# Writing a batch's projection of messages behind the first block of the next batch's messages

## The chip, the cores and the metric

The kernel runs on one core of one Trainium2 chip. The metric is the device time of one execution in microseconds (us); it was measured in three runs of the kernel before. A profile of one further execution shows where that time lies. Engines are named as in the profile: PE is TensorE's matrix unit, PEld its weight loads, DVE the vector engine, ACT the scalar engine, POOL GpSimd, and SP the engine that only issues transfers here.

## The reference, cut to what matters

Four graph layers run over 16 batches of 1024 nodes with 256 features. The change lies in the first one:

```python
m_t = jnp.einsum('uv,bud->bvd', A_m, h_t) * h_t
a_t = jnp.einsum('buv,bud->bvd', S * A_a, h_t)
z_t = beta1 * h_t + beta2 * (jnp.einsum('bvd,de->bve', a_t, Wa) + ba) \
    + beta3 * (jnp.einsum('bvd,de->bve', m_t, Wm) + bm)
```

`m_t` are the messages: a product with the adjacency matrix and then an elementwise product with `h_t`. `S` are scores of the edges, computed from `pre_u` and `pre_v`, two products of `h_t` with halves of `W1`. The term `beta1 * h_t + beta3 * m_t Wm` needs no scores; the kernel computes it ahead of all that does.

## The kernel before, in words

The nodes lie in 8 tiles of 128 partitions, the features in 2 halves of 128. A preparation (to about 103 us) loads the adjacency matrix and makes the edge sides of batches 0 to 3. Then follows the score-free part (generator `score_free`, to about 952 us), in which the change lies, and after it four groups of four batches with the remaining layers.

The score-free part goes over the batches b = 0 to 15. For each of them there are up to four pieces of work on PE:

- `edge_sides` (for b from 4): 8 node tiles, each with a product of 512 columns and one of 256 columns for each feature half, weights `hT`. PE's result lies in two PSUM banks, ACT copies them to `st` (L331, L332), and SP issues three stores for each pair of tiles (L337, L338). `st` has two buffers.
- `messages`: four blocks (feature half dh, node half v), each of 8 products with a bank of 512 columns, 64 matrix instructions in all. Behind each block DVE multiplies the bank by `hT` into `mT` (L351).
- the next batch's input: for b + 1 up to 3 two loads, `h` and its transposed form `hT` (L288, L297); for b + 1 from 4 a load of `h` (L288) and `turned`: 16 transposes on PE into four banks (L308), copied to `hT` in turns by DVE (L139) and ACT (L141). The first bank (v = 0, dh = 0) is copied by DVE, the second (v = 0, dh = 1) by ACT, the third by DVE, the fourth by ACT.
- `without_edges`, the projection: four banks, each of 2 products with weights `wm` and moving operand `mT` (16 matrix instructions), DVE adds `beta1 * hT` into `zb` (L366), and SP stores `zb`, 1 MB (L368). Its first two banks need the blocks of `mT` with v = 0, which are the first and the third; its last two need the second and the fourth.

The order on PE within a batch is thus edge sides, messages, transposes for the next batch, projection; then come the next batch's edge sides. The code is a generator; each `yield` gives an estimate of PE's time since the last one. The helper `Side.along` hands out steps of another generator, `score_steps`, in proportion to it (0.26 steps for each us in this part). A score step is a gather of 512 KB on POOL (L706), two operations on DVE (L823, L825), four on ACT (L829), and one or two scatters on POOL (L711). The first of its DVE operations waits for a matrix product a few instructions back (`paced`), so that the scores can't run ahead of PE. The clearing of a table (32 MB of zero writes, ACT's transfer queue) is also spread over the yields.

The tiles `h` and `hT` share a pool of 5 buffers, `mT` and `zb` one of 4, the PSUM banks one of 8. A buffer goes to the next tile of its pool in order of request. Tile's scheduler sets the order of each engine's instructions from the order of the code, the dependences and a model of times, so loads can stand earlier in SP's queue than in the code.

Of the kernel before, what the change touches and what calls it, by code (L numbers as in the profile page):

```python
# [68 lines left out]
def gnn_stack_kernel(  # L69
# [41 lines left out]
    def bank():  # L111
        return psum[-1].tile([P, HN], F32, tag="bank", name="bank")
# [8 lines left out]
    def paced(ins, back=6):  # L121


        if recent:
            after(tc, ins, [recent[max(0, len(recent) - back)]], mybir.DependencyClass.Sync, "keeps pace")
        return ins

    def product(*args, **kw):
        recent.append(nc.tensor.matmul(*args, **kw))  # L129
        del recent[:-BACK]  # L130
        return recent[-1]
# [15 lines left out]
    def load_wm(pool, queue):  # L147

        wm = pool.tile([P, DH, D], F32, name="wm")
        queue.dma_start(wm, g0_Wm.rearrange("(c p) k -> p c k", p=P))  # L150
        nc.vector.tensor_scalar(wm, wm, beta3, None, ALU.mult)
        return wm

    def load_w1(pool, queue):

        w = pool.tile([P, DH, 3, D], F32, name="w1")
        for s, a in enumerate((g0_W1[:D], g0_W1[D:], g0_Wa)):
            queue.dma_start(w[:, :, s, :], a.rearrange("(c p) k -> p c k", p=P))
        return w

    def with_beta2(w):
        return nc.vector.tensor_scalar(w[:, :, 2, :], w[:, :, 2, :], beta2, None, ALU.mult)
# [54 lines left out]
    def turn_adj(stage):  # L217

        for jt in range(0, NT, 2):
            st = stage(2 * N)  # L220
            for k in range(2):
                for v in range(NV):
                    ps = bank()
                    for c in range(HT):
                        it = v * HT + c
                        nc.tensor.transpose(
                            ps[:, c * P : (c + 1) * P], adj_sb[:, it, (jt + k) * P : (jt + k + 1) * P], ident
                        )
                    evacuate(st[:, k * N + v * HN : k * N + (v + 1) * HN], ps)
                yield 1.2  # L230
            nc.sync.dma_start(
                adjT_d[jt : jt + 2].rearrange("t p v -> p t v"), st.rearrange("p (t v) -> p t v", t=2)
            )

    def load_naturals(stage):

        t = stage(3 * DH * D).rearrange("p (i c k) -> p i c k", i=3, c=DH)
        for i, a in enumerate((g1_W, gat2.W1, gat3.W1)):
            nc.sync.dma_start(t[:, i], a.rearrange("(c p) k -> p c k", p=P))
        return t  # L240
# [43 lines left out]
    def load_h(pool, b, pieces=1):  # L284
        h = pool.tile([P, NT, D], F32, tag="wide", name="h")
        n = NT // pieces
        for t in range(0, NT, n):
            nc.sync.dma_start(h[:, t : t + n, :], x[b, t * P : (t + n) * P].rearrange("(t p) d -> p t d", p=P))  # L288
        return h

    def node_pairs(t):
        return t.rearrange("p (h n) -> p h n", h=DH)

    def load_kept(pools, b):
        h = load_h(pools[0], b)
        hT = node_pairs(pools[0].tile([P, DH * N], F32, tag="wide", name="hT"))
        nc.sync.dma_start(hT.rearrange("p h n -> p (h n)"), hT_d[b])  # L297
        return h, hT
# [41 lines left out]
    def messages(pools, h, hT):  # L340
        mT = node_pairs(pools[1].tile([P, DH * N], F32, tag="wide", name="mT"))
        for dh in range(DH):
            for v in range(NV):
                cols = slice(v * HN, (v + 1) * HN)
                ps = bank()
                for ut in range(NT):
                    product(
                        ps, h[:, ut, dh * P : (dh + 1) * P], adj_sb[:, ut, cols],
                        start=ut == 0, stop=ut == NT - 1,
                    )  # L350
                nc.vector.tensor_tensor(mT[:, dh, cols], ps, hT[:, dh, cols], ALU.mult)  # L351
                yield 6.9
        return mT

    def without_edges(pools, b, hT, mT, wm):

        zb = node_pairs(pools[1].tile([P, DH * N], F32, tag="wide", name="zb"))
        for v in range(NV):
            cols = slice(v * HN, (v + 1) * HN)
            for eh in range(DH):  # L360
                ps = bank()
                for dh in range(DH):
                    product(
                        ps, wm[:, dh, eh * P : (eh + 1) * P], mT[:, dh, cols], start=dh == 0, stop=dh == DH - 1,
                    )
                nc.vector.scalar_tensor_tensor(zb[:, eh, cols], hT[:, eh, cols], beta1, ps, ALU.mult, ALU.add)  # L366
            yield 3.4
        nc.sync.dma_start(zb_d[b], zb.rearrange("p h n -> p (h n)"))  # L368
# [4 lines left out]
    with ExitStack() as stack:  # L373
# [56 lines left out]
        def clear():  # L430

            if zeros:
                paced(nc.scalar.dma_start(zeros.pop(0), zero))
# [252 lines left out]
    with tc.If(listed > 0) as arm:  # L686
        with ExitStack() as stack:
# [214 lines left out]
            def load_gd(g, v, ut, **pace):  # L902
                view = dense[g % BUFS][:DUMP].rearrange("(t p v) b -> t p v b", p=P, v=N)
                gd = gd_pool.tile([P, QN, GB], F32, tag="gd", name="gd")
                ins = nc.sync.dma_start(gd, view[ut][:, v * QN : (v + 1) * QN, :])
                put[g].before(paced(ins, **pace))
                return gd

            def load_hw(b):
                hw = node_major("hw")  # L910
                nc.sync.dma_start(hw, hw_d[b].rearrange("p (t d) -> p t d", t=NT))
                return hw
# [14 lines left out]
            with ExitStack() as first:  # L927
                own1 = first.enter_context(tc.tile_pool(name="own1", bufs=1, reuse_waits="tile"))
                st_pool = first.enter_context(tc.tile_pool(name="st", bufs=2, reuse_waits="tile"))
                side = Side(score_steps(own1))  # L930
                pools = (wide_t, wide_z)
                next_up = load_kept(pools, 0)
                wm = load_wm(own1, nc.sync)
                zero = own1.tile([P, ZERO], F32, name="zero")
                nc.gpsimd.memset(zero, 0.0)

                def stage(n):
                    return st_pool.tile([P, 2 * 3 * D], F32, tag="st", name="stage")[:, :n]

                def score_free():  # L940
                    yield from turn_adj(
                        lambda n: wide_z.tile([P, DH * N], F32, tag="wide", name="stage")
                    )
                    h, hT = next_up
                    for b in range(B):
                        if b == 1:
                            nat = load_naturals(stage)
                            w1 = load_w1(own1, nc.sync)
                        if b == 2:
                            paced(with_beta2(w1))  # L950
                        if b >= GB:
                            yield from edge_sides(st_pool, b, w1, hT)
                        if b == B - 1:
                            first_hw.extend(load_hw(i) for i in range(GB - 1))
                            first_gd.extend(load_gd(0, 0, ut) for ut in range(4))
                        mT = yield from messages(pools, h, hT)
                        now = hT

                        if b + 1 < GB:
                            h, hT = load_kept(pools, b + 1)  # L960
                        elif b + 1 < B:
                            h = load_h(pools[0], b + 1)
                            hT = turned(pools[0], h)
                            yield 2.4
                        yield from without_edges(pools, b, now, mT, wm)
                        if b == 1:
                            prepare(nat)
                            yield 3

                def with_zeros(main):  # L970
                    for n, us in enumerate(main):
                        if 7 < n < 40 or n > 40 and n % 3 == 0:
                            clear()
                        yield us

                side.along(with_zeros(score_free()))
                assert not zeros

# [439 lines left out]
    with arm.Else():  # L1418
        with ExitStack() as stack:
# [7 lines left out]
            w1, wm = load_w1(own, nc.scalar), load_wm(own, nc.scalar)  # L1427
# [80 lines left out]
            with tc.For_i(0, B, 1) as b:  # L1508
                h = load_h(wide, b)
                hT = turned(wide, h)  # L1510
# [35 lines left out]
```

## Time and profile before

| | us |
|---|---|
| three runs: lowest, median, highest | 3159.90, 3167.11, 3171.89 |
| the profiled execution | 3164.07 |
| its span | 3162.6 |
| PE busy | 3092.3 (98%) |
| DVE busy | 2360.7 (75%) |
| ACT busy | 1945.9 (62%) |
| POOL busy | 1876.9 (59%) |

An engine's busy time is the sum of its instructions, overlaps taken once. PE is busy nearly all of the time, so a time of PE without an instruction is what has to be looked for, and next to it what PE waited for. In lists of groups a line gives the line of the program, the engine, the operation with its tiles, the count, the busy time and the mean of one in ns, and then the idle time just before the group's instructions with what released them. In the timeline a line is a stretch of like instructions: its start, its length, and in brackets the idle time before it. All products of the score-free part are issued by one helper, so their line is L129 throughout, and they are told apart by their tiles: `adj_sb,h` are messages, `mT,wm` the projection, `w,hT` the edge sides, `ident,h` (L308) the transposes.

### The profile page before, as it was taken

What the parts mean: (1) busy time and instruction counts of PE and PEld (TensorE: products, weight loads), DVE (VectorE), ACT (ScalarE), POOL (GpSimd) and SP (SyncE); (2) the same over time, 40 slices, a digit from 0 to 9 for tenths busy, and PEclk for the clock granted to TensorE, in tenths of its full rate; (3) what the DMA queues carried; (4) which work ended last, traced back from release to release, by engine and by line L of the source; (5) the groups of instructions that cost most, each with busy time, mean ns of one, the idle gap of its engine ahead of it and who ended that gap; (6) DMA issues with size and microseconds to landing.
All of it is one profiled execution on the core that took longest, in us unless ns stands there. A gap on an engine that the chain in (4) does not pass through costs nothing. (4 is left out here: it accounts for less than half of the span.)

```text
span 3162.6 us, 39016 instructions
## 1 busy us (share of the span) xinstructions
PE 3092.3 (98%) x11954; PEld 2180.8 (69%) x11954; DVE 2360.7 (75%) x3191; ACT 1945.9 (62%) x6512; POOL 1876.9 (59%) x1483
## 2 busy tenths in 40 slices
PE   8999999999999999999999999999999999999999
PEld 5444554544547756888875688888568888858887
DVE  7887778677774678999677899976789982157844
ACT  3245556656667876776887677788767764414242
POOL 1156778676664577767666776766766760076600
PEclk9999999999999999999999999999999999999999
DMA  9988897888889777567877766787765655475500
GB/s 318 331 320 308 271 307 260 269 238 256 249 287 318 227 211 206 154 192 261 286 231 201 211 168 176 255 284 232 221 193 156 167 184 167 134 252 159 164 4 28
DMA packets 288420, 699.96 MB, mean 221 GB/s; under 512 B 46141, under 2 KB 141178, under 8 KB 281034
## 3 DMA queue, kind: packets, MB, share of 16 engines
q0 software_dynamic: 128224, 387.80, 42.0%
q1 hardware_dynamic: 132538, 258.46, 23.8%
q10 hardware_dynamic: 27440, 51.13, 4.3%
q8 instruction: 96, 1.57, 0.2%
q14 instruction: 122, 1.00, 0.1%
HBM read 565.83 MB, written 131.41 MB: 220 GB/s over the span
## 5 line engine op out<-in xcount | busy, mean ns | idle before, releaser
L829 ACT ACTIVATE z<-z 128x256 f32<-128x256 f32 x2432 | 979.0, 406 | 581.8 <-DVE z L825 521.7
L823 DVE TENSOR_TENSOR z<-z,u 128x1024 f32<-128x1024 f32 x608 | 739.9, 1222 | 388.2 <-PE bank L129 250.9
L129 PE MATMUL bank<-feats,m 128*128 128x257 f32 x4096 | 919.5, 382 | 16.1 <-DVE m L1093 10.9
L706 POOL DMA_INDIRECT z<-v_d,slot_v x512 | 654.6, 1278 | 405.1 <-ACT z L829 194.2
L129 PEld LDWEIGHTS bank<-feats,m 128*128 128x128 f32 x4096 | 768.8, 190 | 134.6 <-DVE m L1093 20.8
L711 POOL DMA_INDIRECT dense_d<-gt,slot_at x512 | 680.8, 1330 | 190.8 <-issue 136.2
L825 DVE SCALAR_TENSOR_TENSOR z<-z,w2r 128x1024 f32<-128x1024 f32 x608 | 738.6, 1221 | 9.0
L129 PE MATMUL bank<-gc,hw 128*128 128x256 f32 x2048 | 452.4, 382 | 11.0 <-ACT gc L1121 10.1
L829 ACT ACTIVATION_READ_ACCUMULATOR z<-z 128x1 f32 x2432 | 460.9, 190 | 0.0
L129 PE MATMUL bank<-adj_sb,h 128*128 128x512 f32 x1024 | 442.9, 593 | 3.3 <-DMA h<-in_x_dram 1.6
L129 PEld LDWEIGHTS bank<-gc,hw 128*128 128x128 f32 x2048 | 386.9, 191 | 76.1 <-ACT gc L1121 18.7
L1093 DVE SCALAR_TENSOR_TENSOR m<-rho,tau,adj_sb 128x512 f32<-128x512 f32 x512 | 376.7, 747 | 67.1 <-PE bank L129 64.4
L129 PE MATMUL bank<-adjT_in,y 128*128 128x512 f32 (+1 forms) x960 | 403.9, 581 | 6.1 <-DMA adjT_in<-adjT_d 2.8
L129 PEld LDWEIGHTS bank<-adj_sb,h 128*128 128x128 f32 x1024 | 194.5, 190 | 243.8 <-issue 240.5
L129 PE MATMUL bank<-w,hT 128*128 128x512 f32 (+1 forms) x1024 | 335.5, 488 | 0.9 <-ACT z L829 0.9
L129 PEld LDWEIGHTS bank<-adjT_in,y 128*128 128x128 f32 x960 | 182.0, 191 | 221.6 <-issue 204.5
L1121 ACT ACTIVATE gc<-gd 128x1024 f32<-128x1024 f32 x128 | 265.3, 2073 | 89.4 <-PE bank L129 70.2
L129 PEld LDWEIGHTS bank<-w,hT 128*128 128x128 f32 x1024 | 194.8, 191 | 142.9 <-issue 120.6
L129 PE MATMUL bank<-g_wT,z 128*128 128x257 f32 x1024 | 232.5, 381 | 2.5 <-issue 2.5
L129 PEld LDWEIGHTS bank<-g_wT,z 128*128 128x128 f32 x1024 | 193.2, 191 | 33.2 <-issue 6.3
L706 POOL DMA_INDIRECT z<-v_d,x_node x96 | 121.9, 1270 | 135.1 <-ACT z L829 79.9
L711 POOL DMA_INDIRECT dense_d<-gt,x_at x96 | 121.0, 1261 | 29.3 <-issue 27.1
(169 smaller groups left out, 2327.4 us busy)
## 6 DMA issues: line engine op xcount, KB each, us to landing
gd<-dense_d SPq DMA_DIRECT2D x128, 512.0 KB
dense_d<-zero ACTq DMA_DIRECT2D x64, 512.0 KB
adjT_in<-adjT_d SPq DMA_DIRECT2D x112, 256.0 KB
h<-in_x_dram SPq DMA_DIRECT2D x19, 1024.0 KB
u_d<-st SPq DMA_DIRECT2D x64, 256.0 KB
v_d<-st SPq DMA_DIRECT2D x64, 256.0 KB
hw_d<-st SPq DMA_DIRECT2D x64, 256.0 KB
u<-u_d POOLq DMA_DIRECT2D x32, 512.0 KB
```

What stands on the lines that cost most here:

```text
L129: recent.append(nc.tensor.matmul(*args, **kw))
L706: return nc.gpsimd.indirect_dma_start(out=dst, out_offset=None, in_=src[:], in_offset=bass.IndirectOffsetOnAxis(ap=at, axis=0), **how,)
L711: return nc.gpsimd.indirect_dma_start(out=dst[:], out_offset=bass.IndirectOffsetOnAxis(ap=at, axis=0), in_=src, in_offset=None,)
L823: paced(nc.vector.tensor_tensor(z, z, u, ALU.add))
L825: nc.vector.scalar_tensor_tensor(zk, zk, 0.0, w2r[:, None, :].to_broadcast([P, GB, D]), ALU.max, ALU.mult)
L829: nc.scalar.activation(zk[:, c, :], zk[:, c, :], AF.Copy, accum_out=s[:, k, c : c + 1])
L1093: nc.vector.scalar_tensor_tensor(m, r[:, cols], ta[:, jt : jt + 1], ea[:, jt, cols], ALU.max, ALU.mult)
L1121: paced(nc.scalar.activation(gc, gd.rearrange("p n i -> p i n"), AF.Copy), 16)
```

## The change

The generator of a batch's messages is now run to its first yield, that is through its first block. Then the projection of the batch before it is run in full, and then the other three blocks. A projection is only prepared in its own batch (a generator in the list `behind`) and is run in the next one; the last is run behind the loop. Operands and results are the same, and so are the numbers of instructions and transfers.

```diff
                     h, hT = next_up
+                    behind = []
                     for b in range(B):
...
-                        mT = yield from messages(pools, h, hT)
-                        now = hT
-
+                        steps = messages(pools, h, hT)
+                        yield next(steps)
+                        for last in behind:
+                            yield from last
+                        mT = yield from steps
+                        behind = [without_edges(pools, b, hT, mT, wm)]
                         if b + 1 < GB:
                             h, hT = load_kept(pools, b + 1)
                         elif b + 1 < B:
                             h = load_h(pools[0], b + 1)
                             hT = turned(pools[0], h)
                             yield 2.4
-                        yield from without_edges(pools, b, now, mT, wm)
                         if b == 1:
                             prepare(nat)
                             yield 3
+                    yield from behind[0]
```

## The prediction

> **What bounds the kernel now.** I read the page's busy times first, then PE's groups in the score-free part for what PE waited for, then PE's timeline there, and last what DVE and ACT do at the places where the order changes.
>
> ```profile
> PE 3092.3 (98%) x11954; PEld 2180.8 (69%) x11954; DVE 2360.7 (75%) x3191; ACT 1945.9 (62%) x6512; POOL 1876.9 (59%) x1483
> ```
>
> PE sets the time. What the change can win is idle time of PE in its own part, and the groups of that part (0 to 1010 us) give it:
>
> ```profile
> L129 PE MATMUL bank<-adj_sb,h 128*128 128x512 f32 x1024 | 442.9, 593 | 3.3 <-DMA h<-in_x_dram 1.6 <-ACT st L331 1.5
> L129 PE MATMUL bank<-w,hT 128*128 128x512 f32 x512 | 242.5, 596 | 0.0
> L129 PE MATMUL bank<-mT,wm 128*128 128x512 f32 x256 | 117.5, 611 | 10.2 <-DVE mT L351 10.2
> ```
>
> The projection (`mT,wm`) waited 10.2 us in all for DVE's product `mT`; the edge sides (`w,hT`), which come behind it, waited for nothing. PE's timeline shows where:
>
> ```profile
> 139.59 1.02 PE L129 MATMUL bank<-mT,wm 128*128 128x512 f32 x2
> 142.23 3.70 PE L129 MATMUL bank<-mT,wm 128*128 128x512 f32 x8 [1.61 <-DVE mT L351]
> 149.81 5.49 PE L129 MATMUL bank<-mT,wm 128*128 128x512 f32 x6 [3.88 <-DVE mT L351]
> 155.09 28.04 PE L129 MATMUL bank<-adj_sb,h 128*128 128x512 f32 x64
> ...
> 713.63 4.46 PE L129 MATMUL bank<-mT,wm 128*128 128x512 f32 x10
> 722.75 4.41 PE L129 MATMUL bank<-mT,wm 128*128 128x512 f32 x6 [4.67 <-DVE mT L351]
> ...
> 888.55 1.91 PE L308 MATMUL bank<-ident,h 128*128 128x128 f32 x16
> 890.30 7.03 PE L129 MATMUL bank<-mT,wm 128*128 128x512 f32 x16
> 897.17 20.80 PE L129 MATMUL bank<-w,hT 128*128 128x512 f32 x64
> ```
>
> Batch 0 waits twice, batch 11 once, the other 13 projections not at all: there PE goes from the transposes into the projection (7.03 us) and on into the edge sides without a gap. In those 7.03 us the copies of the new `hT` are made. For the batch turned at 888.55 DVE and ACT show them:
>
> ```profile
> 889.98 1.27 DVE L139 COPY hT<-bank 128x512 f32<-128x512 f32 x2
> ...
> 891.04 0.40 ACT L829 ACTIVATE z<-z 128x256 f32<-128x256 f32 x1
> 891.35 0.19 ACT L829 ACTIVATION_READ_ACCUMULATOR z<-z 128x1 f32 x1
> 891.44 1.05 ACT L141 ACTIVATE hT<-bank 128x512 f32<-128x512 f32 x2
> ```
>
> ACT comes to its copies only behind eight score operations, so the second block of `hT` is there at about 892.0, 1.7 us after PE has ended the transposes at 890.30. Before the change nobody waits for that.
>
> **What the change removes.** In the changed kernel's instruction order PE has, from batch 4 on, 24 message products, 16 transposes, the next batch's edge sides, 8 message products, 8 projection products, and again 24; the scheduler did not undo it. The projection's `mT` is thus more than 20 us old, and its waits go.
>
> Batch 0: from 139.59 to 155.09 are 15.5 us, where a projection takes 6.9 (890.30 to 897.17); 8.6 us were lost. More than the two gaps of 1.61 and 3.88: the six matrix instructions behind the second gap took 5.49 us instead of 6 x 7.03/16 = 2.64.
>
> ```profile
> 144.00:152.00 8.00, 4.12 (x8) 1.73 (x7) 8.00 (x10) 2.78 (x13) 0.89 (x1) 0.82 1.07 335
> 152.00:160.00 8.00, 8.00 (x15) 3.27 (x15) 7.80 (x11) 2.34 (x12) 2.03 (x3) 0.76 1.04 416
> ```
>
> In these windows (length; busy time of PE, PEld, DVE, ACT, POOL; granted clock; DMA share; GB/s) PE's granted clock is 0.82 and 0.76, where it is 1.00 in the windows from 104 to 144: a long gap is paid a second time. Behind the gap of 4.67 six instructions took 4.41, 1.77 too many; behind the gap of 1.61 eight took 3.70, where 3.52 are usual. So a gap near 4 us costs (2.85 + 1.77)/2 = 2.3 us on top, one below 2 us next to nothing. But batch 1's first block now follows at 139.6, and its `h` is not there then: SP's issue of `w` (L158) at 143.06 had waited for the landing of an `h`, and only batch 1's, issued at 120.74, was under way. That is a new wait of 3.5 us; it leaves a gain of 5.1. Bounds: 8.6 if it landed in time, 8.6 - 3.5 - 2.85 = 2.2 if the clock drops. Batch 11: its projection took 713.63 to 727.00, 13.4 us instead of 6.9: 6.5 us won. Together **-11.6 us**.
>
> **What it moves, and the cover that is lost.** Per batch 16 matrix instructions (7.03 us) and four DVE operations `zb` (0.74 each) move behind the next batch's first block; their time stays. The edge sides now stand directly behind the transposes. In the new order their first product (512 columns) and another of 256 columns need only the first block of `hT`, DVE's; the next needs the second, ACT's. A message product of two 512-column instructions takes 2 x 27.70/64 = 0.87, one of 256 columns 2 x 131.7/512 = 0.51, so PE has 1.38 us of cover instead of 7 + 1.38. With 0.1 us for the hand-over (an estimate: DVE's `mT` ended at 722.69 and PE went on at 722.75, and a weight load comes on top), ACT's first copy (0.58) must begin by 0.7 us after the transposes' end. Taken batch by batch, from the end of the transposes to the begin of ACT's first copy and thence to PE's new wait (for batch 12 DVE's first copy, which ends at 723.29, decides):
>
> | batch turned | transposes end | ACT's copy begins | new wait |
> |---|---|---|---|
> | 4, 5 | 256.44, 314.95 | 257.67, 315.96 | 0.5, 0.3 |
> | 6 | 371.67 | 376.18 | 3.8 |
> | 7 | 428.39 | 430.91 | 1.8 |
> | 8 | 485.11 | 490.48 | 4.7 |
> | 9, 10, 11 | 543.46, 600.18, 656.90 | 544.84, 601.08, 658.04 | 0.7, 0.2, 0.4 |
> | 12 | 713.63 | 724.40 | 9.7 |
> | 13, 14, 15 | 776.85, 833.58, 890.30 | 777.87, 834.48, 891.44 | 0.3, 0.2, 0.4 |
>
> The eight short ones make **+3.0 us**; they come from the eight score operations ahead of ACT's copy, which stand there in the changed order too. The four long ones make 20.0, and 6, 8 and 12 are long enough for the clock: 3 x 2.3 = 6.9, together 26.9. They are lags of the score work behind PE: ahead of batch 6's copies DVE waited 1.93 us for a gather, ahead of batch 12's 4.74.
>
> ```profile
> 718.60 1.23 DVE L823 TENSOR_TENSOR z<-z,u 128x1024 f32<-128x1024 f32 x1 [4.74 <-DMA u<-u_d,x_node]
> ```
>
> The yields ahead of each transposition add up as before, so the same score steps stand there; but each long wait of PE also gives the gathers time, and in the part as a whole DVE waited 94 us for PE (40 times), so a lag is not handed on far. Bounds for this term: 0 and 26.9. I take two thirds, as the steps are the same: **+17.9**.
>
> The Trainium skill has a rule that speaks against this exchange (TensorE: Matmul & The Clock Gate, Part 1): the clock falls to half after PE has been idle for a free-running window of about 3.4 us and comes back after as long a busy one. The rows above agree on the point between 1.6 and 3.9 us; by the rule a long wait costs half a window, 1.7 us (an estimate from that page), and the term of three would be 5.1 in place of 6.9, the sum 1.2 lower.
>
> **Queues.** The 15 stores of `zb` (1 MB) that move now stand in SP's queue behind the next edge sides' 12 stores and ahead of the load of `h` two batches on, which waits with them for DVE's `zb`. The load for batch 6 was issued at 293.27; now it follows the projection of batch 3, behind the first block of messages that began at 285.63: 285.63 + 6.9 + 7 + some 2 for DVE is 301.5. It is needed at 369.9, and the slowest such landing above took 143.06 - 120.74 = 22 us: hidden by 46 us, cost 0; only a landing of over 68 us would show. Without the `zb` store just ahead of them the `st` stores land sooner (ACT waited 21.6 us, 9 times, for them), a gain for ACT; but 2 MB, store and load, now move in the second or third block, right ahead of the transposes, where a gather that comes late hurts. At the 284 GB/s of this part that is 7 us of traffic. I take the two as equal; bounds -2 (the two waits of PE for `st` and `z` on ACT, 1.5 and 0.9) and one wait for a gather of the longest kind (5.0) in several batches, priced as a rival. POOL's queue keeps its order of steps. After 952 us nothing changes.
>
> **Sum.** -11.6 + 3.0 + 17.9 = +9.3 on the profiled execution's 3164.1 (span 3162.6 and 1.5 around it), 3173.4. The median of the runs lies 3.0 higher; so 3176, 0.3% above it. I call 0.5% (15.8 us) what a measurement can tell from no change.
>
> **Rivals.** (1) The forecast, the lags come back in part: between +1 and +18.3 (all of them: -11.6 + 3.0 + 26.9), 3171 to 3185; 57%. (2) Not slower: no lag falls on a transposition; only the short waits remain, and 3.0 - 11.6 = -8.6, 3158 to 3163. For it: DVE mostly waits for PE. Against: four of twelve batches had a lag, and the steps are the same. 15%. (3) Clearly slower: the `zb` store and the load of `h` right ahead of the transposes hold up gathers there. A further batch with a lag costs the mean of the four, 20.0/4 = 5.0, and 2.3 for the clock; two more beside all the old ones give 18.3 + 14.6 = +33, 3200. It decides from the point where lags and clock pass 15.8 + 11.6 - 3.0 = 24.4 us in all. For it: DMA is 80 to 95% busy here. Against: in the old order the `zb` store stood right ahead of the `st` stores, for which ACT waited up to 9.1 us. 28%.
>
> The change can't win more than 8.6 + 6.5 = 15.1 us by its own waits, so faster by over 0.5% is 3%. Slower by over 0.5% is the third case and the top of the first, 28% + 12% = 40%; 57% lie within. Range 3158 to 3198; the first case alone 3171 to 3185.
>
> **What would show it.** PE's wait for `mT` gone from 10.2 to near 0; a new idle time of `w,hT` 512 for ACT's and DVE's `hT`, some 15 to 25 us with at least 0.2 in most of 12 batches; the granted clock below 1.00 behind its long ones; a wait of the second batch's messages for `h` near 140 us. I am wrong if `w,hT` still waits for nothing (the copies come sooner than they stood), if the waits there pass 40 us, or if the difference lies after 960 us.

## The result and the profile after

| | before | changed |
|---|---|---|
| six runs each, median (us) | 3163.62 | 3187.09 |
| lowest and highest | 3154.14, 3171.89 | 3179.11, 3192.55 |
| profiled execution, and its span | 3164.07, 3162.6 | 3185.92, 3184.0 |
| score-free part ends (PE's first product for `gc`) | 952.14 | 974.05 |

The changed kernel is slower by 0.81% (ratio 1.0081, 95% interval 1.0068 to 1.0095). Of the 21.4 us between the two spans, 21.9 lie in the score-free part, so nothing is lost or won behind it.

The page's busy times after:

```profile
PE 3097.5 (97%) x11954; PEld 2179.5 (68%) x11954; DVE 2358.1 (74%) x3191; ACT 1947.4 (61%) x6512; POOL 1889.6 (59%) x1483
```

PE's groups of the score-free part (line, tiles, count, busy, mean of one in ns, idle time ahead and its releaser):

```profile
L129 PE MATMUL bank<-adj_sb,h 128*128 128x512 f32 x1024 | 447.5, 595 | 5.4 <-DMA h<-in_x_dram 5.3
L129 PE MATMUL bank<-w,hT 128*128 128x512 f32 x512 | 253.0, 613 | 20.7 <-DVE hT L139 20.7
...
L129 PE MATMUL bank<-mT,wm 128*128 128x512 f32 x256 | 112.5, 592 | 0.0
```

The 10.2 us of waiting for `mT` are gone. In their place the edge sides wait 20.7 us for the copies of `hT`, and their busy time is 10.5 us longer at the same count, most of it (8.6 us, in the four stretches with a long wait below) behind a lower clock. PE's timeline (start, length, stretch, idle ahead) shows where:

```profile
143.23 9.96 PE L129 MATMUL bank<-adj_sb,h 128*128 128x512 f32 x16 [3.38 <-DMA h<-in_x_dram]
153.03 7.03 PE L129 MATMUL bank<-mT,wm 128*128 128x512 f32 x16
...
367.75 1.91 PE L308 MATMUL bank<-ident,h 128*128 128x128 f32 x16
376.99 22.92 PE L129 MATMUL bank<-w,hT 128*128 128x512 f32 x64 [7.33 <-DVE hT L139]
...
439.54 22.37 PE L129 MATMUL bank<-w,hT 128*128 128x512 f32 x64 [3.56 <-DVE hT L139]
...
502.39 23.37 PE L129 MATMUL bank<-w,hT 128*128 128x512 f32 x64 [4.39 <-DVE hT L139]
...
738.30 23.17 PE L129 MATMUL bank<-w,hT 128*128 128x512 f32 x64 [4.92 <-DVE hT L139]
...
974.05 13.98 PE L129 MATMUL bank<-gc,hw 128*128 128x256 f32 x64
```

The long waits stand at the batches turned 6, 7, 8 and 12, the four of the prediction's table. An undisturbed stretch of 64 is 20.80 long; these four are 1.6 to 2.6 longer. The windows after (length; busy PE, PEld, DVE, ACT, POOL; granted clock; DMA share; GB/s), one at batch 1's first block and one at batch 6's edge sides, show the cause:

```profile
144.00:152.00 8.00, 8.00 (x14) 3.32 (x13) 8.00 (x11) 1.71 (x8) 1.02 (x1) 0.69 1.07 333
376.00:384.00 8.00, 7.01 (x15) 3.87 (x16) 6.15 (x7) 5.29 (x21) 6.48 (x6) 0.68 0.66 196
```

The granted clock is 0.69 and 0.68. In the same window from 376 the kernel before had 1.00:

```profile
376.00:384.00 8.00, 8.00 (x24) 4.33 (x23) 7.24 (x9) 4.23 (x19) 6.17 (x7) 1.00 0.74 211
```

Why batch 6's copies came late is read from DVE's timeline:

```profile
372.24 1.23 DVE L823 TENSOR_TENSOR z<-z,u 128x1024 f32<-128x1024 f32 x1 [4.23 <-DMA z<-v_d,slot_v]
373.38 2.35 DVE L825 SCALAR_TENSOR_TENSOR z<-z,w2r 128x1024 f32<-128x1024 f32 x2
375.65 0.68 DVE L351 TENSOR_TENSOR mT<-bank,hT 128x512 f32<-128x512 f32 x1
376.25 1.27 DVE L139 COPY hT<-bank 128x512 f32<-128x512 f32 x2
```

The transposes ended at 369.7, but DVE takes its instructions in order: a score operation waits 4.23 us for its gather, then two more score operations, then `mT` of the last block of messages, then the copies. PE goes on at 376.99, 0.1 us after the first copy. Ahead of batch 8's copies DVE waited 3.76 us for a gather. The lags of batches 7 and 12 began earlier, one or more blocks ahead of the transposes (at 434.08 and 731.47):

```profile
413.34 2.36 DVE L823 TENSOR_TENSOR z<-z,u 128x1024 f32<-128x1024 f32 x2 [11.30 <-PE bank L129]
...
720.86 1.23 DVE L823 TENSOR_TENSOR z<-z,u 128x1024 f32<-128x1024 f32 x1 [5.37 <-DMA u<-u_d,x_node]
```

At batch 12 DVE had waited 5.37 us for a gather, and then 1.01 us for another. At batch 7 it had stood for 11.30 us up to 413.34 and then worked without a pause up to the copies. The trace names a matrix product as what ended that wait, but in experiment 5, with the same kernel, the same operation began 2.8 us into the batch's first block and not 13.6 us; what it waited for here stays open.

The time between the two kernels, from the starts of the transposes (each batch should be 56.72 behind the one before):

| | taken | measured |
|---|---|---|
| batch 0's projection and batch 1's `h` | -5.1 | -2.6 |
| batch 11's projection | -6.5 | -6.5 |
| eight short waits | +3.0 | +4.9 (batch 5 alone 1.9) |
| batches 6, 7, 8, 12 | +17.9 | +29.5 (9.6, 5.3, 7.1, 7.5) |
| the kernel before's own waits for `st` and `z` | 0 | -3.4 |
| sum | +9.3 | +21.9 |

### The profile page after: what moved, and what is told of

Same layout as the page of the kernel before. It is cut to its first block, busy times and chain, and to the rows that moved or that the text cites. A ratio compares the mean times of both kernels' runs of the same rounds, so it can differ in the third digit from the quotient of the medians.

```text
span 3184.0 us, 39023 instructions
## 1 busy us (share of the span) xinstructions
PE 3097.5 (97%) x11954; PEld 2179.5 (68%) x11954; DVE 2358.1 (74%) x3191; ACT 1947.4 (61%) x6512; POOL 1889.6 (59%) x1483
## 5 line engine op out<-in xcount | busy, mean ns | idle before, releaser
L706 POOL DMA_INDIRECT z<-v_d,slot_v x512 | 662.2, 1293 | 418.0 <-ACT z L829 217.3
L129 PEld LDWEIGHTS bank<-feats,m 128*128 128x128 f32 x4096 | 766.2, 190 | 133.8 <-DVE m L1097 21.4
L129 PE MATMUL bank<-gc,hw 128*128 128x256 f32 x2048 | 450.6, 381 | 15.0 <-ACT gc L1125 14.1
L129 PEld LDWEIGHTS bank<-gc,hw 128*128 128x128 f32 x2048 | 384.9, 190 | 80.3 <-ACT gc L1125 24.4
L129 PE MATMUL bank<-w,hT 128*128 128x256 f32 (+1 forms) x1024 | 346.2, 499 | 21.4 <-DVE hT L139 20.7
L331 ACT ACTIVATE st<-bank 128x512 f32<-128x512 f32 x128 | 75.8, 592 | 110.2 <-PE bank L129 92.4
```

The lines of the kernel that those rows point to most:

```text
L331: nc.scalar.activation(st[:, c, :2, :], ps.rearrange("p (s k) -> p s k", s=2), AF.Copy)
L706: return nc.gpsimd.indirect_dma_start(out=dst, out_offset=None, in_=src[:], in_offset=bass.IndirectOffsetOnAxis(ap=at, axis=0), **how,)
```

## The experiments

Theory A is that of the cover: the edge sides now need copies of `hT` for which DVE and ACT have no time left, so the loss is as large as the lag of the score work. The rival (B) is the traffic: store of `zb` and load of `h` together, ahead of the transposes, hold up the gathers. Ratios stand to the kernel before on the same chip, with 95% intervals. Three chips took part: one for the first four experiments, one for the next four, one for the last four; on them the kernel before took 3148 to 3150 us, where it took 3163.62 in the measurement above. The changed kernel itself was run again only beside experiments 6 to 8 (experiment 5), so where experiments 1 to 4 are set against its 20.7 us of waits or its ratio of 1.0081, the comparison goes across chips. `...` in a diff is code of the changed kernel.

**1. The new order for the first three batches alone.** From batch 3 on the projection again follows the transposes.

```diff
                             yield 2.4
+                        if b + 1 >= GB:
+                            yield from behind.pop()
...
-                    yield from behind[0]
```

> The new order for the projections of batches 0 to 2 alone; from batch 3 on the order before. Theory A (the loss is the lost cover of the hT copies): nothing is lost, since no transposes stand in these batches, and batch 0's wait for mT (8.6 us with its clock) is exchanged for a wait for h of 3.4 us and its clock: 1 to 5 us faster than before, ratio 0.998 to 1.000; edge sides wait for nothing, and batch 11's projection may still wait for mT. Theory B (the loss is the traffic of the zb store and the load of h right ahead of the transposes): the same here, as nothing of the traffic moves behind batch 3; it only shows what the first part of the change is worth.

Measured: 3152.20 against 3148.40, ratio 1.0009 (0.9999 to 1.002), above the expected 0.998 to 1.000. The edge sides wait for nothing; the projections from batch 3 on wait for `mT` again (1.86, 3.50 and 0.29). PE's timeline at batch 1's first block:

```profile
143.16 8.67 PE L129 MATMUL bank<-adj_sb,h 128*128 128x512 f32 x16 [3.43 <-DMA h<-in_x_dram]
```

The wait for `h` and the clock behind it (8.67 instead of 7.03) give back a part of what batch 0's waits cost. From the first message product to batch 4's transposes this execution took 138.82 us, and 141.25 to 142.87 in the four profiles with the order of before (before, 2, 9 and 12): some 2 to 4 us are won there, where I had taken 5.1, and the time of the whole kernel is too coarse to show them.

**2. The traffic alone.** The order of the kernel before; only the store of `zb` is held back into the next batch's second block of messages, and the load of `h` behind it.

```diff
-                        mT = yield from messages(pools, h, hT)
+                        steps = messages(pools, h, hT)
+                        yield next(steps)
+                        yield next(steps)
+                        for store in stores:
+                            held_back.append(paced(store()))
+                        mT = yield from steps
...
-                            h = load_h(pools[0], b + 1)
+                            h = load_h(pools[0], b + 1, behind=held_back[b - 3] if b > 4 else None)
...
-                        yield from without_edges(pools, b, now, mT, wm)
+                        stores = [(yield from without_edges(pools, b, now, mT, wm))]
```

> The order of before on PE; only the store of zb is held back into the next batch's messages (behind its second block), and the load of h two batches on stands behind it, as in the changed kernel. Theory A: no loss, since the projection still covers the copies of hT: ratio 0.998 to 1.003. Theory B: most of the loss is here already: ratio 1.004 to 1.009, with waits of PE for mT or hT of 10 us and more in all. Both: indirect transfers on POOL of 4 us and more, which the kernel before has nowhere and the changed kernel has four times just behind such a pair, should show up in this run if the pair of transfers makes them.

Measured: 3151.81 against 3148.40, ratio 1.0014 (1.0005 to 1.0023). The stores were issued 17 to 18 us ahead of the transposes, where they stand 11 to 20 us ahead in the changed kernel. PE waited 7.0 us for `mT`, 3.0 for `st` and none for `hT`. The traffic at its new place costs 1.6 to 7.2 us by the interval, not the 23 us of the first measurement; against the 12 us that the change lost on another chip (experiment 5) that is less clear. In the profile the score-free part isn't longer: from the first message product to `gc` it took 836.4 us, and 835.2 to 840.5 in the profiles of before, 9 and 12.

**3. The copies sooner.** The changed kernel, with the score steps of the last block of messages handed out behind the copies of `hT` instead of ahead of them.

```diff
                 nc.vector.tensor_tensor(mT[:, dh, cols], ps, hT[:, dh, cols], ALU.mult)
-                yield 6.9
+                if (dh, v) != (DH - 1, NV - 1):
+                    yield 6.9
...
                             hT = turned(pools[0], h)
+                            yield 6.9
                             yield 2.4
+                        if not GB <= b + 1 < B:
+                            yield 6.9
```

> The changed kernel, but the score steps that belong to the last block of messages are handed out behind the transposes, so that fewer score operations stand ahead of the copies of hT on ACT. Theory A: the short waits of the edge sides go and the long ones shrink by the 2 to 5 us of these score operations; the wait of the edge sides falls from 20.7 us to 5 to 12, ratio 0.999 to 1.005 against 1.0081 of the change. Theory B: the gathers are as late as before, the waits stay within a few us of 20.7 and the ratio within 1.006 to 1.010.

Measured: 3152.18 against 3148.40, ratio 1.0014 (1.0003 to 1.0024). The waits for `hT` are 7.0 us in all instead of 20.7 (12.7 in experiment 5); the longest, again at batch 12, in PE's timeline:

```profile
722.25 23.70 PE L129 MATMUL bank<-w,hT 128*128 128x512 f32 x64 [3.72 <-DVE hT L139]
```

Traffic and order of PE are those of the changed kernel; the place of the copies among the score steps alone shortens the waits. What is left is DVE being behind from earlier blocks: ahead of batch 12's copies it had waited 4.55 and 1.25 us for gathers. PE waited 3.6 us for `st` besides.

**4. The transposes one block sooner.** The changed kernel, with load and transposes between the third and the last block of messages, so that one block lies between the transposes and the edge sides.

```diff
                             yield from last
+                        yield next(steps)
+                        yield next(steps)
+                        now = hT
+                        if GB <= b + 1 < B:
+                            h = load_h(pools[0], b + 1)
+                            hT = turned(pools[0], h)
+                            yield 2.4
                         mT = yield from steps
-                        behind = [without_edges(pools, b, hT, mT, wm)]
+                        behind = [without_edges(pools, b, now, mT, wm)]
...
```

> The changed kernel, but the next batch's transposes stand ahead of the last block of messages, which then covers the copies of hT for 6.9 us. Theory A: the edge sides wait for 0 to 3 us in place of 20.7, PE has neither the old nor the new wait, and the kernel is 3 to 10 us faster than before: ratio 0.997 to 1.000. Theory B: the traffic still moves in the second and third block, now right ahead of the transposes and their copies; ratio 1.004 and above, with POOL's transfers of 4 us and more and late copies as in the changed kernel.

Measured: 3147.07 against 3148.40, ratio 0.9997 (0.9988 to 1.0005). No wait for `hT` and none for `mT`; the pair of transfers is still there. PE's timeline has two gaps left ahead of 950 us:

```profile
142.94 7.10 PE L129 MATMUL bank<-adj_sb,h 128*128 128x512 f32 x16 [3.43 <-DMA h<-in_x_dram]
...
328.81 7.23 PE L129 MATMUL bank<-w,hT 128*128 128x512 f32 x16 [5.63 <-ACT st L331]
```

The second is a new one. DVE's timeline ahead of it:

```profile
323.85 0.24 DVE L1217 TENSOR_SCALAR to_u<-to_u 128x32 uint32<-128x32 uint32 x1 [13.95 <-DMA extra_d<-xrows,to_u]
```

This instruction belongs to a much later part. The scheduler had moved it far ahead in DVE's order, where it waits for a transfer, and everything behind it stands for 13.95 us. It is there in the kernel before (6.36 us) and in the changed kernel (11.96 us) too.

**5. The changed kernel again,** unedited, on the second chip (that of experiments 5 to 8).

> The changed kernel once more, unedited, beside the three that follow, as the measure for them on one chip. Theory A (lost cover of the hT copies) and theory B (traffic ahead of the transposes) both expect the loss again: ratio 1.005 to 1.010, the edge sides wait for hT for 10 to 25 us, the long waits at batches 6, 8 and 12 if the lags belong to the score steps there, and anywhere if they are chance.

Measured: 3162.29 against 3149.99, ratio 1.0037 (1.0021 to 1.0053), below what was expected. PE waited 12.7 us for `hT`, nearly all of it at batches 6 and 12:

```profile
372.64 23.30 PE L129 MATMUL bank<-w,hT 128*128 128x512 f32 x64 [5.21 <-DVE hT L139]
...
724.99 22.91 PE L129 MATMUL bank<-w,hT 128*128 128x512 f32 x64 [7.05 <-DVE hT L139]
```

The loss is 12 us here and 23 there, and the wait goes with it: batches 7 and 8 had no lag this time. ACT's first copy begins 2.77 us after the transposes' start at both, where it was 6.37 and 7.22.

**6. The pair held back.** The changed kernel; the store of `zb` is issued behind the transposes and the load of `h` behind it, so that the traffic falls into the edge sides.

```diff
-                            h = load_h(pools[0], b + 1)
+                            h = load_h(pools[0], b + 1, behind=held_back[b - 2] if b > 4 else None)
                             hT = turned(pools[0], h)
                             yield 2.4
+                        for store in stores:
+                            ins = store()
+                            held_back.append(paced(ins, 2) if b + 1 >= GB else ins)
...
```

> The changed kernel, but the store of zb and the load of h that stands behind it are held back until the transposes, so that this traffic falls into the edge sides and not into the blocks ahead of the transposes. Theory A: most of the loss stays, ratio 1.004 to 1.008; only transfers on POOL of 4 us and more go, and the long waits at batches 6 and 8 shrink by 2 to 4 us each. Theory B: the loss goes, ratio 0.998 to 1.002, and the edge sides' wait for hT falls to 5 us or less.

Measured: 3165.88 against 3149.99, ratio 1.0052 (1.0035 to 1.0069): as slow as the changed kernel beside it, or slower. PE's timeline:

```profile
376.19 23.79 PE L129 MATMUL bank<-w,hT 128*128 128x512 f32 x64 [4.09 <-DVE hT L139]
```

Store and load were issued 0.3 to 0.7 us ahead of the transposes' start, so this traffic is gone from the blocks ahead of them, and the waits at batches 6 and 12 (there 6.04) remain: 10.6 us in all, beside 12.7. B falls as the main cause.

**7. Experiment 4 without the block on DVE.** The hoisted operation is tied to a recent matrix product, as the score operations are.

```diff
-                nc.vector.tensor_scalar(to_u, to_u, float(XT * P), None, ALU.min)
+                paced(nc.vector.tensor_scalar(to_u, to_u, float(XT * P), None, ALU.min))
```

> The kernel with the transposes ahead of the last block (no wait for mT or hT), and one DVE operation of the last group, the minimum on to_u, held at its own place with a wait for a recent matrix product; the scheduler had drawn it ahead into the score-free part, where DVE stood 14 us behind it until the scatters of the extra rows had landed, and PE waited 5.6 us for st. Theory A with this block as what ate the gain: PE waits no longer for st near 330 us, and the kernel is 6 to 10 us faster than without the edit: ratio 0.996 to 0.9985. Rival: the block is covered by later slack and the gain is lost elsewhere: ratio 0.9985 to 1.0005, as without the edit.

Measured: 3149.53 against 3149.99, ratio 0.9995 (0.9983 to 1.0007), no gain. The wait for `st` is gone, but at batches 7 and 12 ACT's copy began 13.4 and 14.1 us after the transposes' start, more than the one block of messages (6.9 us) that stands between:

```profile
425.35 23.97 PE L129 MATMUL bank<-w,hT 128*128 128x512 f32 x64 [3.75 <-DVE hT L139]
```

PE waited 8.2 us for `hT` in all. One block is too little cover for lags of this size; experiment 4's execution had none above 7.66. Batch 6's lag (8.68) stands here without the block on DVE, so that block isn't what makes it.

**8. Experiment 7, with batch 1's `h` and `hT` loaded sooner,** right behind `wm`.

```diff
                 wm = load_wm(own1, nc.sync)
+                second_up = load_kept(pools, 1)
...
-                            h, hT = load_kept(pools, b + 1)
+                            h, hT = load_kept(pools, b + 1) if b else second_up
```

> As the one before, and the loads of batch 1's h and hT are issued ahead of the stores of the turned adjacency matrix. If the wait for h at 140 us (3.4 us, and up to 2.9 us more for the clock) is what is left of batch 0's loss, it goes and the ratio falls by another 0.001 to 0.002, to 0.994 to 0.997; if the load is slow because of the traffic at that time in general, the wait only moves to the adjacency stores or the first products, and the ratio stays.

Measured: 3153.43 (3145.05 to 3163.79, wide) against 3149.99, ratio 1.0017 (1.0001 to 1.0033); a gain was expected. The wait for `h` is gone, but the product behind it now stands where the kernel before had it:

```profile
156.67 5.49 PE L129 MATMUL bank<-mT,wm 128*128 128x512 f32 x6 [3.94 <-DVE mT L351]
```

In this execution DVE was late with `mT` at batch 0 although PE did a further block first: the earlier `h` moved the wait from one tile to the other. PE waited 2.6 us for `hT` as well.

**9. The kernel before again,** unedited, one execution on the third chip.

> The kernel before, unedited, for a profile on the chip of the runs beside it: how much PE waits for mT there, and how far ACT's copies of hT lag behind the transposes. Theory A (lost cover), with the lags being the score work's and so changing with the chip: where the changed kernel lost less than on the first chip (ratio 1.0037 against 1.0081), the lags behind the transposes are shorter here: two or three of them over 2 us, in place of four. Rival: the lags stand as on the first chip, and the smaller loss has another cause. Ratio 1.000 either way.

Measured: 3148.33; the median of the others there is 3149.90. From the transposes' start to ACT's first copy there were seven lags of more than 3.6 us (4.93, 3.61, 9.89, 4.28, 7.28, 6.32, 6.99), not fewer than the four in the profile of before (6.26, 4.27, 7.11, 12.52); PE waited for no `hT`, as it had the projection to do. Lags of this size are thus common in the old order too, and shorter lags, which were expected here, don't explain why the changed kernel lost less on the second chip; the kernel before has no profile from that chip itself.

**10. The transposes two blocks sooner.** Experiment 7 with one step fewer ahead of the transposes: they stand behind the second block, and two blocks (13.9 us) cover the copies.

```diff
                             yield from last
                         yield next(steps)
-                        yield next(steps)
                         now = hT
```

> The kernel with the transposes sooner and the minimum on to_u at its place, now with two blocks of messages behind the transposes (13.8 us of cover and 1.4 more) in place of one. Theory A with lags of up to 11 us: the edge sides wait for hT for less than 1 us in all where one block left 8.2, PE has left only the wait for h near 140 us, and the ratio is 0.995 to 0.9985. Rival: PE's own part gains, but what comes behind 950 us takes it back, or the lag is passed on to another wait (st, or a PSUM bank that DVE has not read): ratio 0.9985 to 1.001.

Measured: 3141.96 against 3149.90, ratio 0.9972 (0.9962 to 0.9983): faster than the kernel before, and by its ratio than the changed kernel, which was not run on this chip. No wait for `hT`, `mT` or `st` is left. PE's timeline at batch 6, and the end of the part:

```profile
349.39 1.91 PE L308 MATMUL bank<-ident,h 128*128 128x128 f32 x16
351.14 13.90 PE L129 MATMUL bank<-adj_sb,h 128*128 128x512 f32 x32
364.87 20.80 PE L129 MATMUL bank<-w,hT 128*128 128x512 f32 x64
...
937.21 13.98 PE L129 MATMUL bank<-gc,hw 128*128 128x256 f32 x64
```

From the first message product to `gc` the part took 827.7 us, 7.5 to 12.8 less than in the four profiles with the order of before; the medians differ by 7.9. But the longest lag of this execution, from the transposes' start to ACT's first copy, was 5.59 us, which one block would have covered as well: that two blocks hold against lags like experiment 7's follows from their 13.9 us and is not seen here.

**11. Fewer score steps.** The changed kernel with 0.23 score steps for each us instead of 0.26, one execution.

```diff
-PACE = dict(free=0.26,
+PACE = dict(free=0.23,
```

> The changed kernel with 0.23 score steps for each us of the score-free part in place of 0.26; the others run later. Only the part itself is to be read. Theory A with the lags being score work that falls behind PE: the long waits of the edge sides for hT shrink, the sum of that wait falls to under 8 us, the short ones stay, and the part ends 5 to 15 us sooner than in the changed kernel (960.5 on one chip, 974.1 on the other). Rival (the lags come from late gathers alone, whatever the pace): waits of 10 us and more in all.

Measured: 3255.06. The wait for `hT` falls to 0.8 us and the part ends at 945.09, as A has it: with less score work per us, and so with fewer gathers, DVE is not behind (no lag above 3.56). The steps not taken are missing later. PE's groups over the whole span:

```profile
L129 PE MATMUL bank<-gc,hw 128*128 128x256 f32 x2048 | 453.0, 383 | 115.3 <-ACT gc L1125 112.1 <-DVE z L1148 2.4 <-ACT st L1321 0.6
```

These products waited 115.3 us where the changed kernel has 15.0: the score work has to be done in the score-free part.

**12. The kernel before without the block on DVE,** with the diff of experiment 7 alone.

> The kernel before with the minimum on to_u held at its own place, and nothing else: what that block is worth where the projection covers the copies. The block is covered: ratio 0.9985 to 1.0005. Rival, it delays st and so PE in the kernel before too: 0.996 to 0.9985.

Measured: 3151.22 against 3149.90, ratio 1.0004 (0.9995 to 1.0013): no difference. The block (6.4 us in the profile of before) is covered there, so the gain of experiment 10 comes from the order. How much of it belongs to the projection's new place and how much to the earlier transposes is not shown: the kernel before with its transposes two blocks sooner was not run.

## Why the prediction was right in direction and short in size

The time fell into the range and the sign is that of the forecast; the likeliest case's own range ended at 3185, 2 us short, and the loss passed the 0.5% within which I had put most of the chance. On the second chip the same kernel lost 0.37%, inside it. The signs named beforehand came: no wait for `mT`, 20.7 us of waiting for `hT`, a lower clock behind the long waits, a wait for `h` near 140 us.

- **The waits for `mT` go, and batch 11's 6.5 us are won:** right.
- **Batch 0.** The new wait was there (3.38 for 3.5). The choice that the clock does not drop behind it was wrong: 16 instructions took 9.96 instead of 7.03, and 2.6 us were left of 8.6, near the lower bound of 2.2 and not 5.1. In experiment 1's profile this part won 3.8 us against the profile of before, and its whole time shows no gain.
- **The short waits.** Seven of the eight made 2.98 us, for 2.7 in the table; batch 5 added 1.9, of which 0.74 was a wait for `st`; ahead of that the operation of experiment 4 had held DVE for 11.96 us.
- **The long waits: the step that failed, by its size.** The mechanism and the four batches were right, and the waits came to 20.2 us beside 20.0 in the table. But I took two thirds of the term, since a waiting PE gives the gathers time. In sum the waits of PE did not shorten the lags in this execution: waits and clock made 29.5 us, not 17.9. The clock's share was mis-sized too, 8.6 us (four stretches of 20.80 that took 91.83) for 6.9: all four were slowed, by 1.6 to 2.6 us, on average 2.2, near the 2.3 that I had taken for three of them and above the other estimate of 1.7. Batch by batch the table did not hold (7.33, 3.56, 4.39, 4.92 for 3.8, 1.8, 4.7, 9.7), and DVE's first copy ended the wait in all four, where I had gone by ACT's for three. The sum of the four was closer than its parts, by luck. (By the table's own rule batch 12 should have had 10.1, since ACT's copy began at 724.40.) In experiment 5 it was two waits and 12.3 us, so no fixed share of the table would have been right for both: there, and in experiment 6, batches 7 and 8 had no lag behind batch 6's wait, which fits the reason for the two thirds.
- **Waits of the kernel before for `st` and `z`.** I had put them only into the bounds (-2); -3.4 came. The one for `st` was 1.52 to 2.95 us in the profiles with the order of before, 0.74 and 1.15 in the two of the changed kernel.
- **The traffic** was taken as 0. Experiment 2 has it at 1.6 to 7.2 us, and in experiment 6 moving it away won nothing. In the profiled execution four of POOL's transfers were slow behind such a pair, ahead of batches 6 and 8. How much of those two waits is theirs is open; experiment 5 had a wait of 5.21 at batch 6 without one ahead of it.
- **Clearly slower:** lags and clock passed the 24.4 us from which I had called it decided (29.5), so the loss is above 0.5%, but not for the reason given there: batches 6, 7, 8 and 12 are the old lags, no further batch was added, and moving the traffic away (experiment 6) left the loss.
- **The range of the first case** was worked out wrongly at its lower end: a sum of +1 is 3168, not 3171.
- **Not slower:** its condition, that no lag meets a transposition, was not met in either profile of the changed kernel.

Shown is that the lost cover is the cause: more cover (4 and 10 wholly, 7 in part) or less work ahead of the copies (11 almost wholly, 3 in part) takes the waits away, and moving the traffic does not. The lags themselves are older than the change: in all five profiles in which the projection follows the transposes (before, 1, 2, 9, 12) ACT's copies of batches 6, 7, 8 and 12 began 3.61 to 12.52 us after the transposes' start, and 2.6 to 3.1 us where nothing was late. Open is why lags at batches 7 and 8 come in one execution of the changed kernel and not in another, while 6 and 12 were long in both of its profiles.

## What to carry to other kernels

Before moving work on the critical engine, ask what it was covering: here 7 us of projection hid copies that two in-order engines made behind their own backlog, and the change traded a wait of 10 us for one of 20. Measure the cover by the longest lag of the filling work in several executions (14 us here), not by the mean. Once that cover was given back by two blocks of messages, the new order beat the old by 0.3%.

## What the runs showed of the hardware that I had not expected

**A gap near 3.4 us costs anything from 0.1 to 3 us.** The same wait for `h` at 141 to 144 us, and the time of the 16 instructions behind it (7.03 undisturbed):

| run | gap | 16 instructions |
|---|---|---|
| 4 | 3.43 | 7.10 |
| 5 | 3.41 | 7.10 |
| 7 | 3.03 | 8.51 |
| 6 | 3.86 | 8.56 |
| 1 | 3.43 | 8.67 |
| 10 | 3.56 | 9.85 |
| 11 | 3.58 | 9.92 |
| changed, first profile | 3.38 | 9.96 |
| 3 | 3.57 | 10.12 |

A gap of 3.03 lost clock and one of 3.43 did not, so no fixed length decides. From 144 to 152 us the granted clock was 1.00 in runs 4 and 5 and 0.69 in the changed kernel's first profile. The Trainium skill (TensorE: Matmul & The Clock Gate, Part 1) has the activity window free-running, so that the point of change depends on where in it the work falls. The table fits that, though no run shows the window itself; the size of the loss goes beyond the estimate of 1.7 us that the prediction took from that page: five of the nine rows lost less, four lost 2.8 to 3.1.

**Indirect transfers on POOL** took 0.97 to 2.0 us around batch 6, but two of them 4.28 and 4.82 behind a store of `zb` and beside a load of `h`. POOL's and SP's timelines of the changed kernel:

```profile
357.55 4.28 POOL L711 DMA_INDIRECT dense_d<-gt,slot_at  x1 [0.30 <-issue]
362.13 4.82 POOL L711 DMA_INDIRECT dense_d<-gt,slot_at  x1 [0.30 <-issue]
```

```profile
356.46 0.33 SPq L368 DMA_DIRECT2D zb_d<-zb  x1
...
357.56 1.50 SPq L288 DMA_DIRECT2D h<-in_x_dram  x1
```

The like was seen twice more in this profile (4.25 and 4.83 at 484 to 493 us), once in experiment 11 (a gather of 4.69), and in experiments 1, 4, 5, 6, 7 and 8 as a scatter to `extra_d` of 4.74 to 5.16 at 199 to 208 us, in 8 with a gather of 4.91 besides. Each began within 1.3 us of such a pair's issue or next to one that did, and the other six profiles have none in the score-free part, though such pairs were issued in all of them. What decides it stays open.
